# A state-space mixer with two expert layers: the state's decay half a step ahead, the norm's factor behind y, three columns set by ACT

## The chip, the cores and the metric

The kernel runs on 1 core of one Trainium2 chip. The metric is the device time of one execution in microseconds (us), as the median of the runs shown. Shorter is better. The program is one launch of about 37,000 instructions on five engines: PE (TensorE, with its weight loads as PEld), DVE (VectorE), ACT (ScalarE), POOL (GpSimd) and SP (SyncE, which only issues transfers).

## The reference, cut to what matters

The input is one sequence of 4096 rows of width 256. Two layers follow each other, and each adds a mixer and a mixture of experts to its normalized input:

```python
xn = layernorm(x);  x = x + mixer0(xn) + experts0(xn)      # 16 experts, 4 per row, 2 shared
xn = layernorm(x);  x = x + attention1(xn) + experts1(xn)  # 8 experts, 2 per row
```

The change lies in `mixer0` alone, a state-space mixer with 32 heads of 64 values and one group of B and C of 128 values:

```python
gate, hBC, dt = split(xn @ W_in.T + b_in)
h, B, C = split(silu(conv4(hBC)))              # causal, 4 taps, zeros in front of the first row
dt = softplus(dt + dt_bias);  a = -exp(A_log) * dt
state[t] = exp(a[t]) * state[t-1] + B[t] (h[t] dt[t])      # for each head
y[t] = C[t] state[t] + D h[t]
g = y * silu(gate)
out = g * rsqrt(mean(g * g) + eps) * norm_w @ W_out.T + b_out
```

The reference computes the recurrence in chunks. So does the kernel, with chunks of 128 rows.

## The kernel before, in words

**Blocks, steps, halves.** The mixer's 4096 rows are 16 blocks b of 256 rows (`TB`), and each block is two chunks of 128 rows: chunk c = 2b + j, with j = 0 or 1. The 32 heads are four groups gi of eight (`GH`). A step n is one group of one block, in the order (b, gi). A half is one chunk of a step, and the main loop `for k, (n, j) in enumerate(half)` runs over 128 halves, k = 2n + j. So j = 0 is the even half, a step's first chunk, and eight halves make a block.

**What a half holds.** The stages are software-pipelined. In half k the loop records, in this order: the output `late(k - 1)` of the half before (PE `py` L558, then DVE `g` L569); `advance` (below); parts of the projections for the next steps (`tapped`: PE `pj` L360, ACT `cv` L368, three DVE taps L370; `gated`: PE `pg` L430, ACT `gate` L437; `convolved`: ACT `hc` L381); `masked` (two POOL products `mm` L514); `gate_y(k - 1)` (POOL `g` L1016); for half k + 1 `inputs` (PE `pth` L491, DVE `hdt` L495, POOL `hd` L504); `project` of half k - 3 (ACT square `g2` L584, POOL sum `g2` L588, PE `po` L592); and the scans `decays` for half k + 1 (DVE L465 and L469).

**The state.** `advance` multiplies B of the chunk with `hd` on PE (`pst` L527). On POOL it multiplies the old state by the chunk's decay (`state` L534, 128x512). On DVE it adds the two (`state` L540). Each group has two state buffers. The first chunk has no old state, and the last chunk needs no new one. That leaves 120 decays, 60 in even halves and 60 in odd ones.

**The norm.** When `project` has done the last half of block b, `finish(b)` follows in the next half, which is half 8b + 11, an odd one. PE sums the squares (`psq`, 8 products recorded twice, L608), ACT takes the root (`rr` L614), DVE the reciprocal (L615) and the scaled sum (`xb` L617), and SP stores `x_mid`. In `project`, the sum of squares of a half is taken on top of that of the same chunk in the group before.

**The first block.** Its taps reach three columns in front of the first row. `tapped` sets these columns of `pj` to `nb` before the product, 18 times, with a DVE copy of 128x3 (L356).

**PSUM.** `pst`, `psq`, `pth`, the transposed B and the experts' `ptx`, `pgu` and `po0` share two buffers (tag `tr`) in the order of the program. A product that takes a buffer waits until whoever read its last content is done. `pj` and `pg` share three buffers.

**What sets the order.** A planner orders the instructions of each engine, except for those engines that stand under `manual_schedule`, which keep the order of the program. Before the loop SP stands under it. In the loop POOL and SP do. From about half 80 on, all engines do. Three regimes follow. In the first halves, routing for the experts runs on DVE beside the mixer. From half 14 on, POOL sends two indirect scatters of rows a half to the experts (`sends`, L690). From half 80 on, the experts of the first layer run between the mixer's instructions: `ticks`, in most halves two blocks of rows at once, with PE `ptx` L728, `pgu` L744, `po0` L761, ACT L749 and L766, DVE `hid` L751, and on POOL two indirect adds a block (`moe_d` L774). In such a half the loop's points take `ptx`, `pgu`, `po0`, `ptx`, `pgu`, `po0`, the first one right after `advance`; one pair of adds follows `gate_y`, and the other is the last thing in the half.

**After the mixer** (from 1680 us on) come the second layer's norm, its attention and its experts.

Of the kernel before, what the change touches and what calls it, by code (L numbers as in the profile page):

```python
# [10 lines left out]
FP = mybir.dt.float32  # L11
I32 = mybir.dt.int32
AF = mybir.ActivationFunctionType
ALU = mybir.AluOpType
# [4 lines left out]
P = 128  # L19
T = 4096  # L20
NT = T // P
# [3 lines left out]
HP = 64  # L25
# [4 lines left out]
GH = 8  # L30
NG = HEADS // GH
GW = GH * HP
# [34 lines left out]
def last(ap, n):  # L67

    return ap.unsqueeze(len(ap.shape)).to_broadcast([*ap.shape, n])
# [31 lines left out]
def two_layer_kernel(  # L101
# [237 lines left out]
    with tc.tile_pool(name="m", bufs=1) as mp, tc.tile_pool(  # L339
# [10 lines left out]
        def tapped(b, c):  # L350


            pj = mps.tile([P, 512], FP, tag="pj", name=f"pj{b}_{c}", bufs=3)
            h0 = HALO if b == 0 else 0
            if h0:
                nc.vector.tensor_copy(  # L356
                    pj[:, :h0], nb[:, c : c + 1].to_broadcast([P, h0])
                )
            for k in range(KD):
                nc.tensor.matmul(  # L360
                    pj[:, h0 : TB + HALO],
                    w_in[:, k, INTER + c * P : INTER + (c + 1) * P],
                    xts[b][:, k, h0 : TB + HALO],
                    start=(k == 0),
                    stop=(k == KD - 1),
                )
            cv = mp.tile([P, TB], FP, tag="cv", name=f"cv{b}_{c}", bufs=3)
            nc.scalar.activation(cv, pj[:, :TB], AF.Copy, scale=cw[:, c, 0:1])  # L368
            for i in range(1, TAPS):
                nc.vector.scalar_tensor_tensor(  # L370
                    cv, pj[:, i : i + TB], cw[:, c, i : i + 1], cv, ALU.mult, ALU.add
                )
            return b, c, cv
# [107 lines left out]
        def inputs(n, j, hc):  # L481


            b, gi = steps[n]
            c = b * CPB + j
            sl = slice(j * P, (j + 1) * P)
            hs = slice(gi * GH, (gi + 1) * GH)
            tgg = f"{c}_{gi}"
            pth = mps.tile([P, GW], FP, tag="tr", name="pth" + tgg, bufs=2)
            for i in range(CPG):  # L490
                nc.tensor.transpose(  # L491
                    pth[:, i * P : (i + 1) * P], hc[i][:, sl], ident
                )
            hdt = mp.tile([P, GH, HP], FP, tag="hdt", name="hdt" + tgg, bufs=3)
            nc.vector.tensor_tensor(  # L495
                hdt,
                pth.rearrange("p (h q) -> p h q", h=GH),
                last(dt_sb[c // NTP][:, c % NTP, hs], HP),
                ALU.mult,
            )  # L500
            hd = None
            if c < NT - 1:
                hd = mp.tile([P, GH, HP], FP, tag="hd", name="hd" + tgg, bufs=2)
                nc.gpsimd.tensor_tensor(  # L504
                    hd, hdt, last(dec[c // NTP][:, 0, c % NTP, hs], HP), ALU.mult
                )
            return hdt, hd
# [6 lines left out]
                nc.gpsimd.tensor_tensor(m, m, mid(blk["gm"][j], QH), ALU.mult)  # L514
            return mm

        def advance(n, j, blk, hd):

            if hd is None:
                return  # L520
            b, gi = steps[n]
            c = b * CPB + j
            hs = slice(gi * GH, (gi + 1) * GH)
            tgg = f"{c}_{gi}"
            old = state[gi]
            pst = mps.tile([P, GW], FP, tag="tr", name="pst" + tgg, bufs=2)
            nc.tensor.matmul(  # L527
                pst, blk["btok"][j], hd.rearrange("p h q -> p (h q)"), start=True, stop=True
            )
            new = mp.tile([P, GW], FP, tag=f"state{gi}", name="state" + tgg, bufs=2)  # L530
            if old is None:
                nc.vector.tensor_copy(new, pst)
            else:
                nc.gpsimd.tensor_tensor(  # L534
                    new.rearrange("p (h q) -> p h q", h=GH),
                    old.rearrange("p (h q) -> p h q", h=GH),
                    last(dec[c // NTP][:, 1, c % NTP, hs], HP),
                    ALU.mult,
                )
                nc.vector.tensor_tensor(new, new, pst, ALU.add)  # L540
            state[gi] = new

# [459 lines left out]
        side.close()  # L1002
        ordered.close()
        half = [(n, j) for n in range(len(steps)) for j in range(CPB)]
        made, ys, gs = {0: inputs(0, 0, hcs[0])}, {}, {}

        def late(k):
# [34 lines left out]
        for k, (n, j) in enumerate(half):  # L1042
# [36 lines left out]
            late(k - 1)  # L1079
            ahead()  # L1080
            old = state[steps[n][1]]
            ahead_of = projections(conv, gate)
            at_once = ticks is not None
            if at_once:
                advance(n, j, blk, made[k][1])
            next(ahead_of, None)
            point()
            if not at_once:
                advance(n, j, blk, made[k][1])
            ys[k] = old, masked(n, j, blk)  # L1090
            gate_y(k - 1)
            if t:
                next(ticks[3])
            if over:
                finish(over.pop())
            next(ahead_of, None)
            point()
            next(ahead_of, None)
            if k + 1 < len(half):
                n1, j1 = half[k + 1]  # L1100
                made[k + 1] = inputs(n1, j1, hcs[n1])
            point()
            next(ahead_of, None)
# [474 lines left out]
```

## Time and profile before

| what | value |
|---|---|
| median of 3 runs | 2389.88 us (2385.66, 2389.88, 2394.96) |
| the profiled execution's own time | 2384.37 us |
| its span, first to last instruction | 2382.7 us |
| mean granted clock of PE | 0.97 |
| busy in the span: PE, PEld | 2205.6 us, 1749.7 us |
| busy in the span: DVE, ACT, POOL | 1464.8 us, 928.0 us, 1495.6 us |
| mixer with routing on DVE | about 100 to 284 us |
| mixer with scatters on POOL | 284 to 929 us |
| mixer with experts (ticks) | 929 to 1680 us |

The profiled execution lies 5.5 us under the median. Times of single instructions come from it. PE, DVE, ACT and POOL each work through their own queue in order, so an instruction that waits holds all that are queued behind it on its engine. "[1.64 <-DVE state L540]" in a timeline row says that the engine stood idle for 1.64 us before this row, and that the end of the DVE instruction of line 540 released it.

### The profile page before, as it was taken

To read this page: it belongs to the slowest core of one execution; us is meant where nothing else is said; L and a number is where in the kernel's file an instruction comes from. 1 tells how busy PE (TensorE), PEld (TensorE's weight loads), DVE (VectorE), ACT (ScalarE), POOL (GpSimd) and SP (SyncE) were. 2 spreads that over 40 slices of the span, in tenths; PEclk is the share of its full clock that TensorE was granted. 3 is DMA by queue.
4 is the path that set the end of the run, shared out by engine and by line. 5 is a ranking of instruction groups with operands and counts; after the bars stand their busy time and mean duration, and the time that the engine had idled before them with its cause. 6 is when DMAs were issued, how large, how long until landed. Compare 5 with 4: busy or idle time off the path is not lost.

```text
span 2382.7 us, 37115 instructions
## 1 busy us (share of the span) xinstructions
PE 2205.6 (93%) x12840; PEld 1749.7 (73%) x12840; DVE 1464.8 (61%) x3369; ACT 928.0 (39%) x1922; POOL 1495.6 (63%) x1300
## 2 busy tenths in 40 slices
PE   6787999999999998999999999999799999999998
PEld 5565777777777776787777778788465578888887
DVE  6799988988888886565555656677266441111111
ACT  5633343334333333444444434444226722222222
POOL 0345699988988987677788777887421732222222
PEclk8899999999999999999999999999899999999999
DMA  9576689444444445677767767665622457777774
GB/s 313 184 228 197 212 247 258 157 139 153 153 144 137 151 139 157 159 191 169 182 170 192 184 157 186 177 168 120 228 76 69 144 193 189 202 190 201 192 200 115
DMA packets 249979, 418.48 MB, mean 176 GB/s; under 512 B 41793, under 2 KB 186689, under 8 KB 244801
## 3 DMA queue, kind: packets, MB, share of 16 engines
q1 hardware_dynamic: 199920, 352.79, 47.5%
q0 software_dynamic: 43200, 57.83, 13.9%
q10 hardware_dynamic: 6672, 5.51, 0.7%
q8 instruction: 102, 1.67, 0.3%
q14 instruction: 85, 0.69, 0.1%
HBM read 298.73 MB, written 117.31 MB: 175 GB/s over the span
## 4 chain that ended last, share of the span: by engine, by line
PE 37%; POOL 18%; issue 14%; DMA 13%; DVE 11%; ACT 5%; SPq 1%; POOLq 0%; ACTq 0%; DVEq 0%
DMA out<-ys,ids 6%; PE pgu L744 5%; PE pj L360 5%; PE py L558 4%; PE po L592 4%; PE pg L430 3%; POOL mm L514 3%; POOL xg_d L690 3%; DMA moe_d<-ys,ids 3%; POOL state L534 3%; POOL out L1488 3%; DVE cv L370 2%; PE pb L1294 2%; PE po L761 2%; POOL g L588 2%
## 5 line engine op out<-in xcount | busy, mean ns | idle before, releaser
L370 DVE SCALAR_TENSOR_TENSOR cv<-pj,cw,cv 128x256 f32<-128x256 f32 x864 | 403.5, 479 | 96.9 <-ACT cv L368 88.0
L514 POOL TENSOR_TENSOR mm<-mm,btok 128x512 f32<-128x512 f32 x256 | 341.3, 1431 | 12.3 <-DVE mm L465 11.5
L465 DVE TENSOR_TENSOR_SCAN mm<-mm,eyes 128x256 f32<-128x256 f32 x512 | 318.8, 671 | 24.2 <-ACT eyes L471 24.2
L1488 POOL DMA_INDIRECT out<-ys,ids x78 | 120.2, 1541 | 324.5 <-ACT ys L1484 290.7
L360 PE MATMUL pj<-xt,w_in 128*128 128x259 f32 (+1 forms) x1152 | 312.3, 396 | 12.2 <-DVE pj L356 8.7
L430 PE MATMUL pg<-xt,w_in 128*128 128x256 f32 x1024 | 279.9, 395 | 35.6 <-ACT gate L437 32.9
L774 POOL DMA_INDIRECT moe_d<-ys,ids x158 | 248.8, 1575 | 92.7 <-DMA moe_d<-ys,ids 42.2
L360 PEld LDWEIGHTS pj<-xt,w_in 128*128 128x128 f32 x1152 | 216.2, 194 | 79.8 <-issue 35.0
L1472 DVE TENSOR_TENSOR hid<-silu,pu 128x512 f32<-128x512 f32 x78 | 53.7, 688 | 348.6 <-PE pu L1466 348.6
L592 PE MATMUL po<-w_o,g 128*128 128x256 f32 x1024 | 258.3, 385 | 0.0
L430 PEld LDWEIGHTS pg<-xt,w_in 128*128 128x128 f32 x1024 | 188.1, 195 | 93.7 <-ACT gate L437 43.2
L368 ACT ACTIVATE cv<-pj,cw 128x256 f32<-128x256 f32 x288 | 135.4, 471 | 232.7 <-PE pj L360 231.2
L504 POOL TENSOR_TENSOR hd<-hdt,dec 128x512 f32<-128x512 f32 x124 | 142.6, 1150 | 120.8 <-DVE hdt L495 116.4
L592 PEld LDWEIGHTS po<-w_o,g 128*128 128x128 f32 x1024 | 191.8, 193 | 27.3 <-issue 2.9
L1016 POOL TENSOR_TENSOR g<-g,gate 128x512 f32<-128x512 f32 x128 | 179.9, 1405 | 48.8 <-DVE g L569 28.0
L381 ACT ACTIVATE hc<-cv,bw 128x256 f32<-128x256 f32 x256 | 129.2, 505 | 162.6 <-DVE cv L370 162.4
L744 PE MATMUL pgu<-xgt,w 128*128 128x256 f32 x632 | 157.0, 393 | 14.3 <-DVE state L540 14.2
L584 ACT ACTIVATE g<-g 128x512 f32<-128x512 f32 x128 | 80.8, 632 | 203.9 <-POOL g L588 148.5
L469 DVE TENSOR_TENSOR cs<-cs,eyes 128x512 f32<-128x512 f32 x248 | 159.7, 674 | 0.0
L569 DVE SCALAR_TENSOR_TENSOR g<-hc,ch,py 128x128 f32<-128x128 f32 x512 | 144.7, 343 | 21.7 <-PE py L558 21.5
L558 PE MATMUL py<-cs,state 128*64 128x128 f32 x1984 | 143.4, 283 | 12.9 <-issue 9.8
L1466 PE MATMUL pg<-xgt,w 128*128 128x256 f32 x624 | 153.8, 379 | 0.7 <-ACT xgt L1452 0.7
(243 smaller groups left out, 4090.9 us busy)
## 6 DMA issues: line engine op xcount, KB each, us to landing
mm<-step_d SPq DMA_DIRECT2D x128, 512.0 KB, 5.0
cs<-from_d SPq DMA_DIRECT2D x124, 512.0 KB, 5.9
w<-in_w_ffn SPq DMA_DIRECT2D x39, 1024.0 KB, 6.0
w<-in_w_ffn SPq DMA_DIRECT2D x79, 384.0 KB, 3.3
xg_d<-blank SPq DMA_DIRECT2D x26, 828.0 KB, 8.8
xg<-xg_d SPq DMA_DIRECT2D x79, 260.0 KB, 4.3
w<-in_w_ffn SPq DMA_DIRECT2D x39, 512.0 KB, 6.5
xg<-xg_d SPq DMA_DIRECT2D x39, 268.0 KB, 3.2
```

The costliest lines, as they stand in the source:

```text
L360: nc.tensor.matmul(pj[:, h0 : TB + HALO], w_in[:, k, INTER + c * P : INTER + (c + 1) * P], xts[b][:, k, h0 : TB + HALO], start=(k == 0), s ...
L370: nc.vector.scalar_tensor_tensor(cv, pj[:, i : i + TB], cw[:, c, i : i + 1], cv, ALU.mult, ALU.add)
L430: nc.tensor.matmul(pj[:, :TB], w_in[:, k, c * P : (c + 1) * P], xts[b][:, k, HALO:], start=(k == 0), stop=(k == KD - 1),)
L465: nc.vector.tensor_tensor_scan(m, m, eye, 0.0, ALU.mult, ALU.add)
L469: nc.vector.tensor_tensor(m, m, mid(c_in[:, j, :], QH), ALU.mult)
L514: nc.gpsimd.tensor_tensor(m, m, mid(blk["gm"][j], QH), ALU.mult)
L558: nc.tensor.matmul(py[(h % 2) * HP : (h % 2 + 1) * HP, h // 2, :], left[:, h, :], right[:, h, :], start=(a == 0 and h < 2), stop=(a == len ...
L592: nc.tensor.matmul(po[:, j, :], g[:, i, :], w_o[:, k, :], start=(k == 0 and j == 0), stop=(k == NCI - 1), skip_group_check=True,)
L744: nc.tensor.matmul(pgu[:, a, :], w[:, o : o + P], xgt[:, k, :], start=(k == 0), stop=(k == KD - 1),)
L774: nc.gpsimd.indirect_dma_start(out=moe_d[:, :], out_offset=bass.IndirectOffsetOnAxis(ap=ids[:, j : j + 1], axis=0), in_=ys[:, j, :], in_of ...
L1016: nc.gpsimd.tensor_tensor(gs[k], gs[k], gates[n][:, :, j * P : (j + 1) * P], ALU.mult)
L1488: nc.gpsimd.indirect_dma_start(out=out, out_offset=bass.IndirectOffsetOnAxis(ap=ids[:, j : j + 1], axis=0), in_=ys[:, j, :], in_offset=Non ...
```

## The change

There are three edits.

- The decay of the state is a function of its own, `decayed`. For an odd half it is recorded where it was, shortly ahead of `advance`. For an even half it is recorded in the half before, ahead of `inputs`, so on POOL it stands in front of `hd` of the same half instead of behind it. Between the two stand, in the old order, the sum of squares L588 (in three of four even halves) and, where there are any, two scatters or two adds.
- `finish` moves from behind `gate_y` to the front of `advance`, right behind the output `late(k - 1)`.
- The three columns of the first block are set by ACT.

```diff
@@ tapped
             if h0:
-                nc.vector.tensor_copy(
-                    pj[:, :h0], nb[:, c : c + 1].to_broadcast([P, h0])
-                )
+                nc.scalar.copy(pj[:, :h0], nb[:, c : c + 1].to_broadcast([P, h0]))
...
-        def advance(n, j, blk, hd):
+        def decayed(n, j):
+
+            b, gi = steps[n]
+            c = b * CPB + j
+            if c == NT - 1:
+                return None
+            new = mp.tile([P, GW], FP, tag=f"state{gi}", name=f"state{c}_{gi}", bufs=2)
+            if state[gi] is not None:
+                nc.gpsimd.tensor_tensor(
+                    new.rearrange("p (h q) -> p h q", h=GH),
+                    state[gi].rearrange("p (h q) -> p h q", h=GH),
+                    last(dec[c // NTP][:, 1, c % NTP, gi * GH : (gi + 1) * GH], HP),
+                    ALU.mult,
+                )
+            return new
+
+        def advance(n, j, blk, hd, new):
...
-            new = mp.tile([P, GW], FP, tag=f"state{gi}", name="state" + tgg, bufs=2)
-            if old is None:
+            if state[gi] is None:
                 nc.vector.tensor_copy(new, pst)
             else:
-                nc.gpsimd.tensor_tensor(
-                    new.rearrange("p (h q) -> p h q", h=GH),
-                    old.rearrange("p (h q) -> p h q", h=GH),
-                    last(dec[c // NTP][:, 1, c % NTP, hs], HP),
-                    ALU.mult,
-                )
                 nc.vector.tensor_tensor(new, new, pst, ALU.add)
@@ the main loop
+        new_state = decayed(0, 0)
         made, ys, gs = {0: inputs(0, 0, hcs[0])}, {}, {}
...
             old = state[steps[n][1]]
+            if over:
+                finish(over.pop())
+            new = new_state if j == 0 else decayed(n, j)
             ahead_of = projections(conv, gate)
             at_once = ticks is not None
             if at_once:
-                advance(n, j, blk, made[k][1])
+                advance(n, j, blk, made[k][1], new)
             next(ahead_of, None)
             point()
             if not at_once:
-                advance(n, j, blk, made[k][1])
+                advance(n, j, blk, made[k][1], new)
             ys[k] = old, masked(n, j, blk)
             gate_y(k - 1)
             if t:
                 next(ticks[3])
-            if over:
-                finish(over.pop())
...
             if k + 1 < len(half):
                 n1, j1 = half[k + 1]
+                if j1 == 0:
+                    new_state = decayed(n1, j1)
                 made[k + 1] = inputs(n1, j1, hcs[n1])
```

The number of instructions of each engine stays as it is, but for the 18 copies that move from DVE to ACT and one activation-table load fewer on ACT (85 instead of 86), which the planner's order saves. Where the planner orders, the order also changes elsewhere, above all in the first block.

More of the change, by code (lines that the diff above doesn't have):

```diff
@@ L522, in advance @@
             c = b * CPB + j
[L523 to L526, printed above, removed]
+            pst = mps.tile([P, GW], FP, tag="tr", name=f"pst{c}_{gi}", bufs=2)
             nc.tensor.matmul(
```

## The prediction

> **What bounds the kernel now.** First the page: part 1, and the shares in 40 slices (60 us each).
>
> ```profile
> PE 2205.6 (93%) x12840; PEld 1749.7 (73%) x12840; DVE 1464.8 (61%) x3369; ACT 928.0 (39%) x1922; POOL 1495.6 (63%) x1300
> PE   6787999999999998999999999999799999999998
> DVE  6799988988888886565555656677266441111111
> POOL 0345699988988987677788777887421732222222
> ```
>
> PE is the fullest engine, but in slices 2 to 5 DVE and in slices 6 to 15 POOL are as full. So I asked for the windows (busy us and counts of PE, PEld, DVE, ACT, POOL, then clock, DMA share, GB/s):
>
> ```profile
> 120.00:140.00 20.00, 14.02 (x64) 9.77 (x62) 20.00 (x47) 5.29 (x11) 6.98 (x6) 0.91 0.56 156
> 651.00:733.00 82.00, 75.50 (x526) 59.23 (x525) 69.36 (x154) 31.07 (x67) 71.61 (x69) 1.00 0.45 145
> 1300.00:1400.00 100.00, 96.56 (x602) 77.98 (x603) 61.60 (x131) 44.15 (x112) 79.98 (x61) 0.98 0.73 180
> ```
>
> Three regimes: until 265 us DVE has no gap; until 929 us no engine is full, and the queues hand waits round; in the ticks PE has hardly a gap. Next the waits in the ticks (930 to 1600 us; total us, times, longest):
>
> ```profile
> DVE state L540 <- POOL state L534: 37.1, 20, 3.1
> PEld pgu L744 <- DVE state L540: 18.2, 11, 2.5
> PE pgu L744 <- DVE state L540: 14.2, 9, 2.1
> PEld psq L608 <- DVE state L540: 12.4, 4, 3.5
> PE psq L608 <- DVE state L540: 11.4, 4, 3.3
> ```
>
> PE stands for 14.2 + 11.4 = 25.6 us because the state's sum comes late, and that because of POOL's decay. The timeline shows how, first in half 82 (even), then in half 83 (with a finish):
>
> ```profile
> 978.47 1.57 POOL L774 DMA_INDIRECT moe_d<-ys,ids  x1 [0.30 <-issue]
> 979.48 1.63 POOL L534 TENSOR_TENSOR state<-state,dec 128x512 f32<-128x512 f32 x1
> 981.14 0.69 DVE L540 TENSOR_TENSOR state<-state,pst 128x512 f32<-128x512 f32 x1 [2.28 <-POOL state L534]
> 981.88 1.99 PE L744 MATMUL pgu<-xgt,w 128*128 128x256 f32 x8 [1.64 <-DVE state L540]
> ...
> 996.80 1.64 POOL L534 TENSOR_TENSOR state<-state,dec 128x512 f32<-128x512 f32 x1
> 998.48 0.69 DVE L540 TENSOR_TENSOR state<-state,pst 128x512 f32<-128x512 f32 x1 [2.77 <-POOL state L534]
> 999.22 2.66 PE L608 MATMUL psq<-ones,g 128*128 128x1 f32 x16 [3.00 <-DVE state L540]
> ```
>
> The decay stands behind two adds; `pgu` and `psq` want the `tr` buffer that `pst` holds until the sum.
>
> **The ticks, part by part.** Of the nine waits of `pgu`, those at 981.9, 1084.9, 1221.8, 1255.2, 1388.9 and 1492.0 us are in even halves (82, 88, 96, 98, 106, 112): 1.64 + 1.61 + 1.35 + 1.17 + 0.88 + 1.53 = 8.2 us. There the decay now precedes `hd`, and the sum waits for `pst` alone (half 82: `pst` ends at 978.06, the sum could be done at 978.8). The other three (2.06 + 1.84 + 2.08 = 6.0 us) are in odd halves, whose decay stays.
>
> The four waits of `psq` (11.4 us) go: it now takes its buffer ahead of `pst`. Then `pgu` wants the one of `pst`. In half 83 `py` ends at 993.86; then come `psq` 2.66, `pst` 1.12, `pj` 1.04, `ptx` 0.60 and `pg` 1.03, so `pgu` starts at 1000.3, after the sum (999.17). If PE is already 1.64 ahead from half 82, `pgu` waits 0.5. `psq` itself needs POOL's sum of squares, which ended at 991.91. On DVE the reciprocal, the sum `xb` and then the state's sum queue behind the root: 996.5 + 0.26 + 0.15 + 0.87 = 997.8, before POOL's decay. On ACT the root goes ahead of `cv`; its table load fits into the 2.99 us for which ACT stood there.
>
> What is late next: `hd` comes one decay later (1.04 to 1.64 us by L534), and `pst` is queued for it. In nearly all even halves `hd` ends 2 to 7 us before `pst`; in half 114 `pst` already waits 1.36, so up to 1.6 more. In half 126 the same is covered by a wait for `mm` (2.1 us). Sum of squares and adds also move back by one decay, partly into the 0.7 to 2.1 us for which adds wait for landings. So odd sums come no earlier, and of what PE gains in an even half about 0.5 is lost in the odd wait behind it (halves 89, 97). By groups of halves: 82 and 83 give 4.1 (of 4.6), 88 to 91 4.4, 96 to 99 3.9, 104 to 107 4.2, 112 to 115 a loss of 0.5. Sum: -16. Bounds: all 19.6 at best; psq's 11.4 alone if every later `hd` costs what the earlier decay gave.
>
> **The middle (284 to 929 us), eight blocks of 82 us.** Here finish costs. POOL's sum of squares ends late, and `psq` now stands ahead of `pj`, `pst` and `pg`:
>
> ```profile
> 716.80 1.04 PE L558 MATMUL py<-mm,hdt 128*64 128x128 f32 x16
> 719.80 1.28 POOL L588 TENSOR_TENSOR g<-g,g 128x512 f32<-128x512 f32 x1
> 721.13 1.05 PE L608 MATMUL psq<-ones,g 128*128 128x1 f32 x8 [0.57 <-POOL g L588]
> ```
>
> Had `psq` stood behind `py` (end 717.85), its first eight products would end at 718.8, and PE would wait for 721.1: 2.3 instead of 0.57 us, 1.7 more a block, with `pj`, `pst`, `pg` and the transposes queued behind. On ACT the order of the changed program puts the root, and one square (L584) ahead of the Silu load, `gate` and the next `cv`. That square wants the gated `g` of POOL, done at 727.25; so `gate` (before at 724.99) ends near 729.2 and `cv` near 729.6, and DVE, which has the taps of that `cv` queued in front of two scans and `g`, stands for some 1.9 us.
>
> Against this stands POOL's own chain. In halves 56 to 60 POOL is full, its order is what paces: in half 56 it stood 0.97 us ahead of `hd`, which the decay (1.05) now fills. What follows comes up to 0.5 us earlier; more is cut off by `hdt` (697.87 against 698.40 of `hd`). With 0.5 in hand the late `cv` still reaches POOL's `g` at 735.2 (before 735.5), and the wait of `psq` is absorbed, since PE stood 1.57 us at 736.56 in any case. In half 62 the decay stands before `hd` without a gap to fill (0.10): the sum of squares comes 0.95 later, ACT's square behind it, the next `cv`, DVE's tap (which stood 2.06 for it) and so the next `hd`. So a block gains 0.3 and loses 0.95: +0.65. In four of the eight blocks ACT's new order takes one `cv` out from behind that square, worth up to 1.7; I set these at -0.5. Sum: 4 x 0.65 - 4 x 0.5, near +1; I take +2, as waits rather add than cancel. Bounds: -4 (0.5 a block, kept everywhere) and +21 (1.7 + 0.95 a block, nothing absorbed).
>
> **The first block.** 18 copies of 0.155 us leave DVE (L356). 13 of them lie behind 85 us, where DVE has no gap: -2.0. The others lie where ACT leads (19.5 of 25 us busy between 60 and 85). ACT's price is not in the trace; its nearest rows are the cast of 128x2 (0.20) and the root of 128x2 (0.26), and I take 0.20 as that, too, is a copy. Some nine of them stand in ACT's busy part: 1.8 us, less one table load (1.28), +0.5, which the bound by DVE behind it may hide. Behind each copy on ACT `cv` and `gate` are queued, as is PE's `pj`; ACT is idle there for 14 us of 20. I take -2, and -6 to +6 as bounds: DVE's copies held PE for 8.7 us and POOL's `g` for 17.5, and the planner has rewritten the order of all three.
>
> [...] Here the load takes 1.28 (722.12 to 723.40) and the root starts at 723.41. [...]
>
> SP's list is the same, instruction by instruction; the store of `xb` merely starts earlier.
>
> **Sum.** -16 + 2 - 2 = -16 us. The profiled execution took 2384.4 (span 2382.7 and 1.7 around), which would become 2368.4; it lies 5.5 under the median 2389.9, and I apply the difference to that: 2373.9.
>
> **Rivals.** (1) Slower: the middle is held by `psq` and by ACT's square. 1.7 on PE, 0.95 on `hd`, 1.9 on DVE: 4.55 us a block if they add up, 36 in eight. With -18 from the rest that gives 2408. From 2.25 a block on nothing of the gain is left. For it: ACT already waits 89.5 us for L588 between 400 and 820 us, and PE 17.3 for `gate`. Against it: PE, ACT and DVE all have gaps there, in which a shift ends. Chance 0.1.
> (2) POOL takes the gain of the even halves back: `hd` and the adds pass one decay on, and PE waits at `pst` or `mm` instead of `pgu`. Left are psq's 11.4, less what odd halves lose (some 3), and +2 - 2: 2381. For it: in the halves 82, 88, 96 and 112 POOL reached `hd` 2.0 to 2.5 us after `hdt`. Against it: `pst` comes 2.3 to 2.8 us later still. Chance 0.24.
> (3) It doesn't do what it says: the sum waits as long as before, since `pst` or DVE's queue takes the decay's place, and `pgu` inherits the wait of `psq`. Then only the first block is left: 2388. Chance 0.1.
> (4) More: the odd waits fall as well, since POOL's products, now right behind the adds, start up to 1.6 us earlier: 6.0 more and nothing given back, with the middle at 0: about 2364. Chance 0.1.
>
> **How the numbers follow.** My forecast has 0.46, and 2374 is its value; by itself it reaches from 2367 to 2381. The range 2360 to 2393 takes in the rivals but the slow one: the low end is 2389.9 - 19.6 - 4 - 6, rounded; the high end psq's gain alone, with 1.7 a block lost in the middle, 2389.9 - 11.4 + 13.6, and 1 for the median. A measurement tells 0.5% from no change, that is 12 us: faster is below 2378, slower above 2402. Of the forecast 0.40 lies below 2378, of rival 2 0.06, and rival 4 wholly: 0.56. Slower is most of rival 1: 0.09. The rest is 0.35.
>
> **What would show it.** Right: no `psq` or even `pgu` behind the state's sum in the ticks, DVE's 37.1 us for POOL's decay halved, `psq` waiting some 2 us for POOL's sum in each middle block at an unchanged 82 us a block, DVE full up to 263 us. Wrong: middle blocks of 84 us or more; or `pst` waiting for `hd` in half after half of the ticks; or odd `pgu` waits that have grown by what the even ones lost.

## The result, and the profile after

| | kernel before | changed kernel |
|---|---|---|
| median of 13 runs each | 2391.05 us | 2405.44 us (2392.23 to 2411.95) |
| ratio, 95% interval | | 1.0048 (1.0028 to 1.0068) |
| profiled execution, its span | 2384.4, 2382.7 us | 2412.0, 2410.1 us |

The forecast was 2374. By the ratio the change costs about 11 us (the medians lie 14.4 apart). The profiled execution of the changed kernel is the slowest of its 13, so the 27 us between the two spans overstate it, and every stage below was profiled in other runs too. First the page, busy us after the change:

```profile
PE 2217.6 (92%) x12840; PEld 1760.1 (73%) x12840; DVE 1465.1 (61%) x3351; ACT 930.7 (39%) x1939; POOL 1496.1 (62%) x1300
```

DVE has its 18 copies less and ACT 18 more; POOL has the same 1300 instructions. PE was 12 us longer busy (2205.6 before) with the same 12840 products, PEld 10; no other engine got fuller by more than 3 us; so the loss is in waits and in PE's speed. The table divides both traces at the ends of `hdt` of the halves 16, 80, 112 and 127 (us between them; the second profile of the changed kernel is the run a2 below):

| stretch | before | changed | changed, again |
|---|---|---|---|
| start to `hdt` 16 (first blocks) | 284.4 | 292.7 | 292.5 |
| `hdt` 16 to 80 (the middle) | 657.8 | 668.3 | 666.6 |
| `hdt` 80 to 112 (ticks) | 538.6 | 544.1 | 534.6 |
| `hdt` 112 to 127 | 179.6 | 182.0 | 180.2 |
| behind the mixer | 722.2 | 723.0 | 763.8 |

(The kernel before was timed again beside each group of runs and took 2383 to 2429 us. That difference lies behind the mixer: 719 to 726 us in the groups where it took 2383 to 2391, 757 to 764 where it took 2424 to 2429. So each run is compared with the kernel before as timed beside it.)

**The middle.** The windows of the middle, before and then changed (busy us of PE, PEld, DVE, ACT, POOL, then clock, DMA share, GB/s):

```profile
284.43:942.18 657.75, 611.73 (x4196) 480.36 (x4190) 557.03 (x1225) 251.49 (x538) 575.06 (x543) 0.98 0.54 169
```

```profile
292.73:961.07 668.34, 618.00 (x4188) 488.82 (x4182) 556.29 (x1225) 253.64 (x538) 576.16 (x544) 0.96 0.52 166
```

Of the 10.6 us, 6.3 are PE *busy* longer with the same products (618.0 against 611.7), and only 4.3 are idle. The column to see is the granted clock: 0.96 for 0.98. Summed over the trace's record of the granted clock, (1 - share) x time is 25.6 us here and 10.2 us before; I call this the lost clock. A finish half shows where it comes from: PE's timeline in half 43, and windows of 2 us over the same time:

```profile
567.84 1.05 PE L612 MATMUL psq<-ones,g 128*128 128x1 f32 x8
569.88 1.05 PE L612 MATMUL psq<-ones,g 128*128 128x1 f32 x8 [0.98 <-POOL g L592]
570.79 1.17 PE L358 MATMUL pj<-xt,w_in 128*128 128x259 f32 x4
571.76 1.91 PE L538 MATMUL pst<-hd,btok 128*128 128x512 f32 x2
573.46 1.86 PE L428 MATMUL pg<-xt,w_in 128*128 128x256 f32 x4
```

```profile
568.00:570.00 2.00, 1.01 (x9) 0.93 (x10) 2.00 (x5) 0.27 (x2) 1.93 (x3) 1.00 0.20 76
570.00:572.00 2.00, 2.00 (x13) 1.88 (x14) 1.54 (x5) 1.97 (x3) 1.74 (x2) 0.93 1.02 415
572.00:574.00 2.00, 2.00 (x4) 0.88 (x4) 0.39 (x2) 0.54 (x2) 2.00 (x3) 0.50 0.44 175
```

`psq` waits 0.98 us for POOL's sum of squares; a wait there was foreseen. What was not foreseen stands behind it: from 571.7 to 575.1 us PE has half its clock, `pst` takes 1.91 us (1.12 in the ticks at full clock) and `pg` 1.86 (1.03). In seven of the eight finish halves of the middle (19, 27, ... 75) the clock falls within 12 us of `psq`; in the kernel before in two.

**The ticks.** Waits of PE from `hdt` 80 to `hdt` 112 in the changed kernel:

```profile
PE pgu L748 <- DVE state L544: 30.8, 7, 6.0
```

The waits of `psq` (11.4 us) and of the even `pgu` are gone, as forecast. In their place stand seven waits of 2.3 to 6.0 us, all in odd halves four apart (85, 89, 93, ...). POOL's timeline in half 85, and the DVE sum that PE's `pgu` (at 1050.85 after 5.03 us) waits for:

```profile
1037.64 1.56 POOL L778 DMA_INDIRECT moe_d<-ys,ids  x1 [1.98 <-ACT ids L738]
...
1040.53 1.64 POOL L502 TENSOR_TENSOR hd<-hdt,dec 128x512 f32<-128x512 f32 x1
1045.42 1.56 POOL L778 DMA_INDIRECT moe_d<-ys,ids  x1 [3.26 <-ACT cv L366]
...
1048.43 1.65 POOL L523 TENSOR_TENSOR state<-state,dec 128x512 f32<-128x512 f32 x1
```

```profile
1050.11 0.69 DVE L544 TENSOR_TENSOR state<-state,pst 128x512 f32<-128x512 f32 x1 [5.67 <-POOL state L523]
```

`hdt` was done at 1036.15, yet `hd` starts 4.4 us later: POOL is behind. It stands still at the adds (1.98 and 3.26 us). By the code, an add waits until the adds of the block before have landed, and the ACT names there are only the last semaphores seen. The traces bear this out where they have the landing of the add before: of the adds that stood over 0.6 us in this stretch, 42 of 44 in the kernel before and the changed one start 0.7 to 0.85 us behind it, 14 of 15 of those named ACT among them. The runs with two sums below test it.

**The first blocks.** PE's waits for the three columns between 85 and 300 us, before and changed:

```profile
PE pj L360 <- DVE pj L356: 8.7, 6, 3.5
```

```profile
PE pj L358 <- ACT pj L356: 10.3, 6, 6.3
```

PE waits longer for ACT's copies than it did for DVE's, 1.6 us in sum, 6.3 us at once.

### The profile page after: what moved, and what is told of

The parts are those of the page before. It is cut to its first block, busy times and chain, and to the rows that moved or that the text cites. A ratio compares the mean times of both kernels' runs of the same rounds, so it can differ in the third digit from the quotient of the medians.

```text
span 2410.1 us, 37088 instructions
## 1 busy us (share of the span) xinstructions
PE 2217.6 (92%) x12840; PEld 1760.1 (73%) x12840; DVE 1465.1 (61%) x3351; ACT 930.7 (39%) x1939; POOL 1496.1 (62%) x1300
## 4 chain that ended last, share of the span: by engine, by line
PE 41%; POOL 18%; issue 13%; DMA 11%; DVE 10%; ACT 5%; SPq 1%; POOLq 0%; ACTq 0%; DVEq 0%
DMA out<-ys,ids 6%; PE pgu L748 6%; PE pj L358 5%; PE py L562 4%; PE po L596 4%; PE pg L428 4%; POOL mm L512 3%; POOL xg_d L694 3%; PE pst L538 3%; PE po L765 3%; POOL out L1496 2%; DVE cv L368 2%; PE pb L1302 2%; POOL g L592 2%; DVE mm L463 2%
## 5 line engine op out<-in xcount | busy, mean ns | idle before, releaser
L512 POOL TENSOR_TENSOR mm<-mm,btok 128x512 f32<-128x512 f32 x256 | 344.3, 1455 | 16.8 <-DVE mm L463 14.5
L358 PE MATMUL pj<-xt,w_in 128*128 128x259 f32 (+1 forms) x1152 | 320.8, 404 | 15.0 <-ACT pj L356 10.3
L358 PEld LDWEIGHTS pj<-xt,w_in 128*128 128x128 f32 x1152 | 221.3, 199 | 85.5 <-issue 33.8
L502 POOL TENSOR_TENSOR hd<-hdt,dec 128x512 f32<-128x512 f32 x124 | 148.7, 1199 | 105.9 <-DVE hdt L493 103.0
L748 PE MATMUL pgu<-xgt,w 128*128 128x256 f32 x632 | 161.2, 401 | 30.9 <-DVE state L544 30.8
L748 PEld LDWEIGHTS pgu<-xgt,w 128*128 128x128 f32 x632 | 124.4, 200 | 53.0 <-DVE state L544 34.0
L588 ACT ACTIVATE g<-g 128x512 f32<-128x512 f32 x128 | 80.8, 632 | 205.9 <-POOL g L592 151.5
L435 ACT ACTIVATE gate<-pg,b_ch 128x256 f32<-128x256 f32 x256 | 120.3, 470 | 92.5 <-PE pg L428 90.9
```

The costliest lines, as they stand in the source:

```text
L358: nc.tensor.matmul(pj[:, h0 : TB + HALO], w_in[:, k, INTER + c * P : INTER + (c + 1) * P], xts[b][:, k, h0 : TB + HALO], start=(k == 0), s ...
L502: nc.gpsimd.tensor_tensor(hd, hdt, last(dec[c // NTP][:, 0, c % NTP, hs], HP), ALU.mult)
L748: nc.tensor.matmul(pgu[:, a, :], w[:, o : o + P], xgt[:, k, :], start=(k == 0), stop=(k == KD - 1),)
```

## The experiments

The expectations name theories by letters: A (POOL's queue with its landings paces the ticks, `psq`'s wait and clock cost the middle, the ACT copies the head), and rivals B to K as they are introduced.

### One part at a time

e1: the decay alone. e2: finish alone. e3: the copies alone. e4: decay and finish.

```diff
@@ in short; e1, e2, e3 against the kernel before; e4 against the changed kernel
+e1:  if j1 == 0: new_state = decayed(n1, j1)       # ahead of inputs(n1, j1, ...)
+e2:  if over: finish(over.pop())                   # behind late(k - 1), ahead()
+e3:  nc.scalar.copy(pj[:, :h0], nb[...])
+e4:  nc.vector.tensor_copy(pj[:, :h0], nb[...])
```

> Only the even halves' state decay is taken ahead of hd; finish stands where it stood and DVE sets the three columns. Theory A (in the half blocks with ticks GpSimd's queue, with its scatter adds that each wait for the block before to land, is as long as TensorE's half; the stall of finish was the time in which GpSimd caught up, and with finish moved PE waits at pgu instead; the first block's loss is the ACT copies): this run keeps finish's stall and the DVE copies, so head 0 against before, middle 0 to +4 (pst waits for an hd that is one decay later), ticks -2 to -8 (the even halves' pgu waits, 14 us in the profile of before, fall by about half): 2383 to 2393 where before has 2391. Rival B (the decay itself is the harm: hd and the second pair of adds are queued behind it and come later): ticks +6 to +10 here, middle +4, 2400 to 2406, with the pgu waits on the state sum at 25 us or more.

> Only finish is moved right behind the half's y; the decay stays with the state's update and DVE sets the three columns. Theory A: head 0, middle +6 to +10 (psq is first in PE's order behind py and waits for GpSimd's sum of squares, 7.8 us in the changed kernel), ticks -2 to +6 (psq's 11.4 us gone, given back at pgu on the state sum, which shows 25 us or more): 2395 to 2407. Rival B (the decay does the harm): ticks -10 to -14, middle +2, 2377 to 2385, pgu's waits on the state sum stay at 14 us or less.

> Only the 18 copies of the first block's three columns go from DVE to ACT. Theory A: PE waits for these copies in ACT's queue; the first y is 6 to 9 us later and nothing behind takes it back: 2397 to 2400 where before has 2391, by the profile all of it ahead of the first state update (hdt of half 16 at +6 to +9). Rival C (the 8 us in the head of the profiled run are the planner's order of that build or one run's scatter, not the copies): within 2 us of before.

> The whole change without the ACT copies. Theory A: 6 to 9 us less than the changed kernel's 2405, that is 2396 to 2399, still 5 to 8 over before; head as before, middle +8 to +12, ticks -4 to +6 with pgu's waits at 25 to 31 us. Rival C (the copies don't matter): 2403 to 2407. The prediction's own sum without its first block would be 2376.

| run | ratio to before (95%) | `hdt` 16 at | middle | lost clock there | ticks 80 to 112 |
|---|---|---|---|---|---|
| e1 decay | 0.9989 (0.9974 to 1.0003) | 285.9 | 658.6 | 8.5 | 534.7 |
| e2 finish | 1.0095 (1.0076 to 1.0114) | 287.6 | 675.0 | 25.6 | 536.8 |
| e3 copies | 1.0017 (1.0004 to 1.0031) | 288.8 | 661.7 | 10.2 | 535.1 |
| e4 decay, finish | 1.0040 (1.0027 to 1.0053) | 287.8 | 670.5 | 23.9 | 533.1 |

Finish is the harm, 23 us of it by the ratio (more than theory A gave it), and it lies in the middle: +17. With the decay it costs less, as POOL's sum of squares then comes earlier: `psq` waits 16.8 us in e2 and 9.1 in e4. Rival B, harm by the decay, is out. The copies cost about 4 us, less than theory A's 6 to 9: in the 14 profiles with DVE copies `hdt` 16 ends between 284.4 and 288.7 (286.9 on average), in the four with ACT copies between 288.8 and 292.7 (291.4). In the whole kernel the ratios don't tell (1.0040 without the copies, 1.0039 and 1.0048 with them), so of their size only the traces speak. How they cost it isn't shown: in e3 PE waited 4.0 us for ACT's copies, less than the 8.7 for DVE's, though its first blocks took 4.4 us longer. What is longer in all four is PE's wait at `py` for DVE's `g` (8.0 to 10.4 us, 1.6 to 7.0 with DVE copies), and the planner's order there differs too.

### The ticks: a second sum for the adds

g1 and g2 send the adds of odd blocks to a second tensor, so that a block's adds wait for the block two before. Nothing reads that tensor, so both leave the odd blocks' share out of the result. g3 keeps the decay and moves finish in the ticks only.

```diff
@@ g1 (kernel before), g2 (changed kernel, DVE copies)
-                        out=moe_d[:, :],
+                        out=(moe_d, moe_e)[m % 2][:, :],
...
-                    parts, before0,
+                    parts, before0[m % 2],
...
@@ g3 (changed kernel, DVE copies)
-            if over:
+            if over and ticks is not None:
```

> The kernel before, with the scatter adds of odd blocks of rows put into a second sum in DRAM that nothing reads (the odd blocks' share of the routed experts is left out of the result). So a block's adds wait for the landing of the block two before it, and no longer for the last one. Theory A (in the stretch with ticks GpSimd's queue sets the pace, and the landing of the adds is what holds it: 80 us of idle ahead of 123 adds between hdt of halves 80 and 112, which took 533 to 544 us in all six profiles whatever the change): the idle ahead of the adds falls by 30 us or more, the stretch takes 515 to 528 us, the whole 10 to 20 us less than before (ratio 0.992 to 0.996). Rival D (the landing is hidden: GpSimd would wait for hdt instead): the idle moves to hd, the stretch stays at 533 to 540 and the whole within 3 us of before.

> The same second sum in the changed kernel with the columns set by DVE (the odd blocks' share is left out here too). Theory A: with GpSimd off the path the prediction's gain in the ticks shows: the stretch from hdt 80 to hdt 112 is 6 to 12 us shorter than in the kernel before with two sums, pgu's waits on the state sum under 10 us; the middle keeps its loss of 10 to 13 us: the whole 0 to +6 us against the kernel before with two sums. Rival D: the stretch within 3 us of that of the kernel before with two sums, 25 us or more of pgu waits, the whole 10 us above it.

> The even decay ahead of hd everywhere, finish behind y only where there are ticks and at its old place in the middle, DVE copies. Theory A (the middle's loss is psq's wait of about 2 us at its new place and the half clock that follows it, 24 to 26 us of lost clock against 10 in before): middle as in the run with the decay alone (658 us from hdt 16 to hdt 80, 9 to 12 us of lost clock), ticks 530 to 535: 3 to 8 us under before, ratio 0.9965 to 0.999. Rival E (the decay and finish together hold the middle by the order of GpSimd and DVE, not by psq's wait): middle 664 to 670, ratio 1.001 to 1.004.

| run | ratio (95%) | ticks 80 to 112 | PE idle there | POOL idle ahead of the adds | middle |
|---|---|---|---|---|---|
| before | 1 | 538.6 | 26.5 | 79.7 | 657.8 |
| g1 | 0.9860 (0.9835 to 0.9885) | 504.4 | 2.9 | 29.2 | 657.8 |
| g2 | 0.9874 (0.9853 to 0.9896) | 496.6 | 2.4 | 29.2 | 665.2 |
| g3 | 0.9998 (0.9982 to 1.0015) | 532.1 | 28.0 | | 658.8 |

POOL's adds in the ticks: of the kernel before, of the changed kernel, and of g1 (its two tensors):

```profile
L774 POOL DMA_INDIRECT moe_d<-ys,ids x123 | 193.8, 1576 | 79.7 <-DMA moe_d<-ys,ids 38.5 <-issue 17.5 <-ACT hc L381 6.8
L778 POOL DMA_INDIRECT moe_d<-ys,ids x122 | 192.3, 1576 | 110.7 <-DMA moe_d<-ys,ids 34.5 <-ACT hc L379 19.6 <-issue 18.0
```

```profile
L775 POOL DMA_INDIRECT moe_d<-ys,ids x62 | 97.7, 1576 | 14.6 <-issue 12.4 <-ACT ids L735 1.6 <-ACT silu L750 0.3
L775 POOL DMA_INDIRECT moe_e<-ys,ids x62 | 97.7, 1576 | 14.6 <-issue 12.1 <-ACT cv L369 2.4
```

The wait for landings is what holds POOL, and POOL holds PE: without it the ticks fall by 34 us though not one product changed. PE's idle goes from 26.5 to 2.9, and PE is 10.6 us less busy, of which the lost clock, 15.4 before and 6.8 in g1, can be 8.6. Rival D is out. The ACT and DMA names in the waits vanish together, so those ACT names did stand for landings. With POOL off the path the change makes the ticks 7.8 us shorter: 504.4 against 496.6 here, 496.8 and 496.5 in two runs below. The windows of the ticks of g1 and g2:

```profile
944.19:1448.62 504.43, 501.46 (x3120) 410.18 (x3121) 318.44 (x677) 236.88 (x585) 417.24 (x316) 0.99 0.76 188
953.42:1450.02 496.60, 494.15 (x3123) 405.22 (x3122) 318.40 (x677) 237.20 (x586) 417.06 (x316) 1.00 0.77 191
```

These 7.8 us are not the waits that the forecast priced, as those are gone in g1 without the change: 0.2 us are left at `pgu`, 0.1 in each `psq`. They are PE's busy time, 501.5 against 494.2. In g1 a stretch of 3.41 us at half clock follows `psq` at its old place in each of the four finish halves; in g2, with `psq` behind `py`, there is none. With the landing waits the ticks are 538.3 us on average over four profiles with the old ticks (538.6, 535.1, 539.2, 540.4) against 535.6 over the five with decay and finish moved (544.1, 534.6, 534.3, 533.1, 532.1): about 3 us, within their scatter.

g3 has the middle of before, which puts the middle's loss on finish at its new place; but it isn't faster than before, against my 3 to 8 us. Its profile adds up to that: the ticks are 6.6 us shorter, the first blocks 3.4 longer, the rest 2.5 longer. The kernel before has the shortest first blocks of all 14 profiles with DVE copies.

### The middle: psq's wait, or ACT's order

g4 is e2 with a `psq` that has nothing to wait for: the norm leaves out the last group.

```diff
@@ g4 (on e2): sq3 is the list of sums as it stands before the last group
-                        psq[:, q : q + 1], blk["sq"][q][:, i, :], ones[:, :1],
+                        psq[:, q : q + 1], blk["sq3"][q][:, i, :], ones[:, :1],
```

> Finish moved as in the run with finish alone, but psq sums the squares of the first three groups only (the last group is left out of the norm), which are ready a half step earlier; so psq has nothing to wait for, and everything else stands where it stood. Theory A: no idle at psq in the middle, lost clock back from 25.6 to 8 to 14 us, the middle 656 to 662 us instead of 675, the whole 2 to 6 us from before instead of 23 over it. Rival F (psq's matmuls of one column lower the clock by themselves behind py, wait or none): lost clock 20 us or more, middle 666 to 672. Rival E (DVE's reciprocal and xb sums ahead of hdt hold it): lost clock falls, but the middle stays at 668 or more.

Measured: 1.0138 (1.0113 to 1.0163), the middle 688.9 us, the lost clock 32.4: worse, a clear miss of all three theories. PE's waits in the middle, e2 and then g4:

```profile
PE pg L430 <- ACT gate L437: 21.3, 24, 2.9
PE psq L615 <- POOL g L595: 16.8, 8, 2.3
```

```profile
PE pg L430 <- ACT gate L437: 42.4, 30, 3.5
PE po L601 <- DVE xb L626: 8.8, 8, 1.1
```

`psq`'s wait is gone and a longer one, 3.5 us in each finish half, stands at `pg`. ACT shows why. With finish moved, the planner puts ACT's square, which waits for POOL's gated `g`, between the root and the Silu load; in half 43 of the changed kernel:

```profile
576.02 0.63 ACT L588 ACTIVATE g<-g 128x512 f32<-128x512 f32 x1 [3.48 <-POOL g L1021]
576.67 1.28 ACT L435 ACT_TABLE_LOAD   x1
```

and in the kernel before:

```profile
558.89 1.28 ACT L437 ACT_TABLE_LOAD   x1
560.18 0.47 ACT L437 ACTIVATE gate<-pg,b_ch 128x256 f32<-128x256 f32 x1
```

The gate comes 11.7 us behind `hdt` of the half, where the kernel before has the load right behind the root (end 558.87) and the gate at 8.0. So PE meets two late things side by side, and taking one away bares the other. q1 is e2, q2 is g4, c1 the kernel before and c3 the changed kernel, each with this one square of a block on DVE; p2 is the kernel before with no root on ACT (the square root is left out), whose planned order puts the square ahead of the gate with finish at its old place.

```diff
@@ q1, q2, c1, c3
-            nc.scalar.activation(g2, g, AF.Square)
+            if gi == 1 and j == 0 and 0 < b < 10:
+                nc.vector.tensor_tensor(g2, g, g, ALU.mult)
+            else:
+                nc.scalar.activation(g2, g, AF.Square)
@@ p2
-            nc.scalar.activation(rr, psq[:, :CPB], AF.Sqrt, bias=eps_t, scale=1.0 / INTER)
+            nc.vector.tensor_scalar(rr, psq[:, :CPB], 1.0 / INTER, EPS, ALU.mult, ALU.add)
             nc.vector.reciprocal(rr, rr)
```

> The run with finish alone, and in blocks 1 to 9 the one square (first chunk, second group) that ACT's order had put between the root and the Silu table load is taken by DVE. ACT's order after the root is then cv, table load, gate, as in the kernel before. Theory G (finish moved in the middle costs because that square, which waits for GpSimd's gated g, now holds the table load and both gates on ACT, and PE at pg): gates near 8 us behind hdt again instead of 12, middle from hdt 16 to hdt 80 658 to 665 us instead of 675; psq's wait of about 2 us a block may stay. Theory H (it is psq's wait and the half clock behind it): middle 671 to 676, as without this edit.

> As the run before this one, and psq sums the first three groups only (the last one is left out of the norm), so that it waits for nothing. Theory G: the run with psq's wait taken away took 689 us in the middle because PE then met the late gate in full (3.5 us a block at pg); with the square gone from ACT it takes 655 to 660, lost clock 8 to 14, the whole within 4 us of before. Theory H as well has 655 to 660 here, but not in the run before this one; if it stays at 670 or more, both fall, and what is left is DVE's reciprocal and sums ahead of hdt.

> The kernel before with finish at its old place, but the factor worked out by DVE alone, mean plus eps and its reciprocal (the square root is left out): ACT has no root and no table loads there, and its order then has the same square ahead of the gate, though finish has not moved. Theory G: pg waits for the gates 1 to 3 us a block more, middle 664 to 680 instead of 658, although ACT has less to do and psq waits as little as before. Theory H: middle 653 to 658, nothing lost.

> Control: the kernel before, and only the one square of a block goes from ACT to DVE; there it stands behind both gates. Theory G (that square costs only where it stands ahead of the gates): middle 654 to 659 us as before, the whole within 3 us. Rival K (it also costs at its old place, because cv and hc are queued behind its wait for GpSimd, and the runs with finish moved gained from this too): middle 640 to 650, the whole 8 to 18 us less; then those runs are to be compared with this one, and moving finish still costs 6 to 16 us in the middle by psq's wait and the clock.

> The changed kernel whole, and only that square on DVE. Theory G: ACT's order after the root is as in the kernel before, the middle 650 to 658 us instead of 668, the head keeps its 4 to 8 us for the ACT copies, the ticks 530 to 544: ratio to before 0.996 to 1.001, 10 to 18 us less than the changed kernel. Theory H (psq and clock alone): middle 664 to 670, ratio 1.002 to 1.006.

> The changed kernel once more, beside the two others. All theories: ratio to before 1.003 to 1.007, middle 666 to 672 with 22 to 27 us of lost clock. What it tells: its first profile had ticks of 544 us where the same code without the ACT copies had 533. If the landings of the adds set that (theory A), the number scatters and comes to 530 to 546 here without any change of code; if the ACT copies shift the ticks for good, it is 542 to 546 again. Head: 4 to 9 us over before at hdt 16.

Middle in us (lost clock), and the ratio to before:

| finish | square on ACT | square on DVE |
|---|---|---|
| old place | before 657.8 (10.2), 1 | c1 642.5 (10.2), 0.9934 (0.9908 to 0.9960) |
| moved, alone | e2 675.0 (25.6), 1.0095 | q1 656.3 (23.9), 1.0002 (0.9985 to 1.0018) |
| moved, no wait at `psq` | g4 688.9 (32.4), 1.0138 | q2 638.7 (3.4), 0.9940 (0.9920 to 0.9960) |
| moved, the whole change | a2 666.6 (22.2), 1.0039 (1.0024 to 1.0054) | c3 653.4 (15.4), 0.9975 (0.9958 to 0.9992) |
| old place, square ahead of the gate | p2 684.1 (32.4), 1.0112 (1.0078 to 1.0145) | |

The windows of the middle of q1 and q2, which differ only in what `psq` reads:

```profile
288.25:944.60 656.35, 616.80 (x4186) 487.95 (x4182) 562.20 (x1234) 249.89 (x530) 576.74 (x543) 0.96 0.52 169
```

```profile
288.17:926.87 638.70, 601.24 (x4192) 474.76 (x4186) 562.22 (x1233) 246.57 (x530) 576.94 (x543) 0.99 0.54 174
```

Without the control I would have named the square as the cause: q1 brings e2 back to the time of before. But c1 gains 15 us from the same edit with finish at its old place (rival K; theory G had 654 to 659). Against its own control, moving finish still costs 13.8 us (642.5 to 656.3), nearly as much as with the square on ACT (17.2). q2 shows what that is: without `psq`'s wait the middle is 17.6 us shorter, of which 15.6 are PE busy less (616.8 to 601.2) at a clock of 0.99, and early finish is then as good as late. So with the square out of the way, the wait and the clock behind it are the whole cost of moving finish. (Three went past the bounds set for them: q1 with 656.3 us, just under G's 658 to 665; q2 with 638.7, against the 655 to 660 of G and H; p2 with 684.1, against G's 664 to 680.) Rival F, one-column products that lower the clock wait or none, falls in the middle with q2's 3.4 us of lost clock.

With the square ahead of the gate, the late gate alone is enough to cost 26 us (p2) or 31 (g4 against before), and much of that is clock as well: PE is busy for 627.6 us in p2 and 622.8 in g4, against 611.7. In the changed kernel the late gate is there, but does not show as a wait. PE's waits for the gate in the middle, before and changed:

```profile
PE pg L430 <- ACT gate L437: 24.9, 29, 3.0
```

```profile
PE pg L428 <- ACT gate L435: 20.1, 24, 2.9
```

And with the square on DVE in both kernels the change costs 10.9 us in the middle (c3 against c1), with the square on ACT 8.8 to 10.6. So there `psq`'s wait and the clock are what costs. c3 and c2 (below), whose middles differ in the place of finish and in little else, show both parts: 653.4 against 640.9 us, of which 7.3 are idle and 5.3 PE's busy time.

What stands ahead of a fall of the clock can be read from the traces. I took, for each of the eight finish halves of the middle, the time from the start of the first to the end of the last product of `psq` and whether the clock fell below 0.93 on the average of the 12 us from that start:

| kernels | `psq`, first to last | clock falls |
|---|---|---|
| e1, g3, q2 (no wait) | 1.8 to 1.9 us | 0 of 8 each |
| before, e3, c1 (at most 0.6 us of wait) | 1.8 to 2.6 us | 2, 1, 3 of 8 |
| the changed kernel, e2, q1, e4, a2, c3 (mostly 1.0 to 2.3 us of wait) | 2.1 to 5.4 us | 7, 8, 6, 7, 7, 5 of 8 |

Of the 48 halves in the last row, the clock fell in 38 of the 41 with 0.98 us of wait or more and in two of the seven with less. Against this, the nine other waits of PE of 1.55 to 1.95 us in the middle of the kernel before (at `pg` and `ptb`) had no fall behind them, and of eleven such waits in e1 two had. Longer ones had falls behind them in g4: each of its nine waits of 2.9 to 3.5 us at `pg` has a stretch at half clock that begins within 2.4 us of its end. So in these runs a wait of 0.98 us or more amid `psq`'s one-column products mostly had a fall behind it (38 of 41), and one of 1.55 to 1.95 us amid wide products mostly had none (18 of 20). The length of the wait is not all of it: in g1's ticks 0.13 us at `psq` had a fall behind it, four times of four (126.3 us apart, 37 times the step that the next paragraph gives, so rather one case than four). Whether the width of the products matters is not shown; no run made them wider.

The falls come at even distances: in the trace of the kernel before and in that of the changed kernel, every stretch at one clock (46 and 56 of them) begins a whole number of steps of 3.41333 us behind the first, to within 2 ns. The stretches at half clock in the middle of the changed kernel last 3.41 or 6.83 us, one or two of these steps. The shortest wait between `psq`'s products with such a stretch behind it there was 0.98 us.

a2: ticks 534.6 with the same code that had 544.1, so 10 us of the first profile were scatter, as theory A has it. c3 shows the head at 291.4 and the middle at 653.4, inside G's 650 to 658; but c1 gains 15 us from the same edit at the old place, so this is rival K again and does not speak for G.

### A version that beats both

b1: g3 with two sums in full, both cleared and both added to the residual. c2: the same with the one square on DVE.

```diff
+    moe_e = dram.tile([T + SPARE, DM], FP, name="moe_e")      # cleared like moe_d
         nc.gpsimd.tensor_tensor(av, av, mo, ALU.add)
+        mo = wk.tile([P, TPB, DM], FP, tag="xs", name=f"me{g}")
+        nc.sync.dma_start(mo, moe_e[g * FB : (g + 1) * FB, :].rearrange("(j p) d -> p j d", p=P))
+        nc.gpsimd.tensor_tensor(av, av, mo, ALU.add)
```

> Nothing left out: the run with finish moved in the ticks only, and the scatter adds go to two sums in DRAM in turn, both cleared beforehand and both added to the residual after the mixer (8 more reads of 512 KB and 8 more GpSimd sums). Theory A (the adds' landings set the pace of the ticks): ticks from hdt 80 to hdt 112 495 to 503 us as in the runs with a second sum that nothing read, the stretch behind the mixer 5 to 20 us longer for the reads: 2360 to 2378 where before has 2383, ratio 0.988 to 0.997. Rival I (the reads and sums delay the start of the second layer's norm by all that the ticks gain): ratio 0.997 to 1.003.

> Nothing left out: the run with two full sums (decay ahead of hd, finish moved in the ticks only, DVE copies), with that square on DVE. Theory G: as that run, ratio 0.984 to 0.988, as finish stands behind the gates in the middle anyway. Rival K: 8 to 18 us less than that run, ratio 0.978 to 0.983.

b1: 0.9859 (0.9833 to 0.9886); c2: 0.9783 (0.9760 to 0.9806), 2375.5 where before has 2429.2. Ticks 496.8 and 496.5; the stretch behind the mixer 769.5 and 769.3 where the kernels timed beside them without the reads had 757 to 764, some 5 to 12 us for them. Rival I is out. The middle of c2:

```profile
288.70:929.60 640.90, 604.66 (x4186) 476.39 (x4182) 563.10 (x1234) 248.69 (x530) 577.74 (x544) 0.99 0.57 180
```

## Why the prediction was wrong, step by step

By stage the runs have about -3 in the ticks, +10 in the middle and +4 in the first blocks, together the 11 us measured, where the forecast had -16, +2 and -2.

- **The ticks, -16: the step that failed.** The waits named did go. But the sum took each as a gain for PE, and counted what POOL gives back as 0.5 here and there. PE ran at POOL's pace, whose adds wait for landings, and finish's stall was time in which POOL caught up; so the waits came back in odd halves (30.8 us at `pgu`). The passage "into the 0.7 to 2.1 us for which adds wait for landings" treated that wait as slack; it grew from 79.7 to 110.7 us in the first profile. g1 shows that all the waits priced hung on it: without it they are gone with no change of order. Measured: about -3. Rival 2 named POOL, but only for the even halves. The sign "odd `pgu` waits that have grown by what the even ones lost" came true.
- **The middle, +2: the step that failed in size.** `psq`'s wait came as priced in e2 (16.8 us in eight halves, 2.1 each, against 2.3), and half as long in the changed kernel, since the decay brings the sum forward. "The wait of `psq` is absorbed, since PE stood 1.57 us at 736.56 in any case" was wrong, and the sum had no term for the clock: in the changed kernel PE was 6.3 us longer busy, and `psq`'s wait grew by 4.3 (3.5 to 7.8). Measured +9 to +11, inside the bounds of -4 to +21. The square ahead of the gate was seen and set to 0 beside POOL's lead; in the changed kernel that holds, but where `psq` waits for nothing (g4), or finish stands at its old place (p2), it costs 31 and 26. The later `hd` had no term here either: in e1 `pst` waited 5.5 us for it (0.2 before), and the waits for the gate fell by 6.9, so the middle stayed.
- **The first block, -2.** The price was right (median 0.164 us a copy against 0.20). What failed is the gain: the sum took DVE's freed time, 2.0 us, as time of the block, which instead ends about 4 us later, inside the bounds of -6 to +6. Which wait carries this stays open; PE's waits for the copies themselves changed by +1.6 us in the changed kernel and by -4.7 in e3.
- **The decay by itself** gave 0.9989 (0.9974 to 1.0003), about -3 us with no change inside the interval, and e1's ticks are 4 us under those of before, but within 1 us of those of e3, which has the old order there: that it gains is not shown.
- **Rival 1** said 2408, and 2405 was measured, but not by its sum: that had 36 us in the middle against 18 gained elsewhere; the runs have about 10 lost there, and elsewhere as much lost as gained.
- **Rival 4** was added up wrong: 19.6 + 6.0 + 2 from 2389.9 gives 2362, not 2364. Nothing else hung on it.

What stays open: what lengthens the first blocks, by ACT's copies (4 us) and by some 4 us among kernels that have the same copies on DVE; and what sets off a fall of the clock.

## What to carry to other kernels

When a stall is to go, ask which queue used it to catch up. Here POOL did, behind an add that waits for a landing, and 34 us lay in that wait while the stalls it caused looked like 25 us of separate things. In this kernel a short wait of PE beside one-column products (0.98 us or more at `psq`) had to be priced with the half clock behind it (38 times of 41); the granted clock in the windows shows it. And a repair needs its control: the same edit on the kernel before, or a gain of its own is taken for the cause.

## What the hardware showed that I had not expected

- The clock fell within 12 us of the start of a `psq` with mostly 1.0 to 2.3 us of wait in it (40 of 48 finish halves of the middle in six kernels; in the changed kernel to half, for 3.41 or 6.83 us), and behind two of twenty waits of 1.55 to 1.95 us between wide products (before and e1).
- The same indirect add took 3.7 to 9.3 us from issue to landing in the changed kernel (median 4.8, of the 60 of 158 whose landing the trace gives). The ticks, which wait for such adds, took 532 to 544 us with the same code there; without those waits 496.5 to 496.8.
- POOL's decay of 128x512 took 1.04 us at its shortest and 1.66 at its longest in one execution of the kernel before; for `hd` in the ticks the mean was 1.07 us in g1 and 1.49 in the changed kernel. No run shows why.
- Behind the mixer the same instructions took 722 us in the profile of the kernel before and 761 in that of e1, taken at another time.
